# A two-layer attention and FFN kernel: the first stack by groups of heads on two DMA queues, the first weights copied on ScalarE, and products of zeros on TensorE

## The chip, the cores and the metric

The kernel runs on one core of one Trainium2 chip. The metric is the device time of one execution in microseconds; the median of the runs shown is compared. A core has TensorE (matrix products, with a separate weight load), DVE (VectorE), ACT (ScalarE), POOL (GpSimd) and SP (SyncE, which here issues the DMAs). The five engines run their own instruction streams in order and wait for each other by semaphores.

## The reference

Eight batches of 512 tokens with 256 channels (`x`) and a context of 512 tokens with 128 channels go through two layers. Every sublayer is added to `x`, and its input is normalised first.

```
x = x + L0_xattn(layernorm(x), ctx)   # causal self attention + cross attention, 16 heads of 16, then Wp
x = x + L0_ffn(layernorm(x))          # rmsnorm, int8 activations and ternary weights, 256-1024-256, gelu
x = x + L1_xattn(layernorm(x), ctx)   # cross attention, 16 heads of 16, then Wo
x = x + L1_ffn(layernorm(x))          # per-tensor int8 activations and weights, 256-1024-256, gelu
```

Attention is softmax(q k^T / 4) v for each head. All inputs and outputs are float32.

## The kernel before

**Units.** The attentions are cut into units: S (self attention of layer 0, causal), C (cross attention of layer 0) and X (cross attention of layer 1), one of each for each batch. A unit has four groups of four heads, numbered G over the whole kernel, and two halves n (u = 0, 1) of two groups each. For every half a chain of jobs runs:

- `ln_job` (line 494) loads `x` (for the first unit the tile `first_x`, loaded at line 330), takes statistics with `stats` (line 469: four `bn_stats` and four `bn_aggr` on DVE, then three small POOL operations), normalises, and transposes by products with the identity into `xlt`.
- `weights_job` (line 432) loads the q and k weights (`raw_*`, line 442; the first two already at line 337) and copies them into the order of the heads (line 449): the first four blocks on DVE, the others on POOL. After the fourth block it waits for the key `("stack", 0)` and loads the five other weights (line 456).
- `prep_job` (line 550) makes q and k of one half on TensorE (`wide`: four products of 32 columns that run side by side). ACT adds the bias, and the result is split into a high float32r part and a low remainder (`qkt`): on DVE for the first two halves (a CAST and a TENSOR_TENSOR each), on POOL after that.
- `stack_job` (line 597) copies `qkt` by six DMAs of 256 KB on SP's queue into `qk`, where every head has its high and low parts on 48 partitions. When it has done so, the keys `("stack", 2n)` and `("stack", 2n + 1)` are set.
- `max_one` (line 668) makes the scores of a pair of heads on TensorE (for S units with a mask added by two small products) and takes row maxima on DVE (`mx`).
- `rows_job` (line 706) waits for the maxima of both groups of a half, splits them into a high and a low part on POOL (`mhl`), transposes them on TensorE, evacuates them as `mrow`, and writes them by two DMAs (line 741) into partitions 48 and 49 of the q side of `qk`. Two rows of ones on the k side, written once by `init_job` (line 1361), take them into the next product.
- `exp_one` (line 756) makes the scores again, now with keys on the partitions and the maximum subtracted by those two rows, and ACT takes the exponential; `av_part` (line 804) multiplies by V.

The feed-forward network of layer 0 runs between them, and that of layer 1 at the end, after all attention.

**Order.** The whole program is written out by a planner at build time. `Plan` keeps a modelled clock for each engine and for the DMA (`run`, `op`, `pe`, `dma`), and `at` holds modelled due times by key. Jobs are generators that yield the time at which they want to go on; `until(key)` waits for a modelled time. The main loop at the end of `build` emits, at the modelled TensorE time, whichever of maxima, exponentials and products with V is ready and most urgent, and jobs between them. The emission order is the order of the instructions on every engine, so a changed due time can change the order of all that follows. The chip doesn't see the modelled times; it sees the order and the semaphores.

**Queues.** All DMAs of the kernel before are issued by SP, in emission order: at the start `x`, two weight blocks, eight small loads of biases (line 369), eight small copies of identity and mask (line 374), then two more weight blocks, then the stacks. `inputs_jobs` (line 1389) goes on to the next inputs (context and the next `x`) once `("stack", 0)` is set, and `init_job` too waits for that key.

**PSUM.** Eight banks are named `bank0` to `bank7`, and in twos `pair0` to `pair3`; `Writer.matmul` (line 259) adds waits when a bank changes its use. Nearly all instructions are recorded at a helper's line: TensorE's at 259, those of DVE and ACT at 241.

## Time and profile before

| | |
|---|---|
| median of 3 runs | 1462.89 us (1462.37 to 1465.43) |
| the profiled execution | 1460.25 us |
| its span, first to last instruction | 1458.4 us |
| mean granted TensorE clock in it | 0.971 |
| TensorE products / weight loads | 1374.8 us (94%) / 597.5 us (41%) |
| DVE / ACT / POOL busy | 1142.0 us (78%) / 1035.5 us (71%) / 681.6 us (47%) |
| DMA moved | 207.03 MB, mean 142 GB/s |
| first 64 us: TensorE / DVE / ACT busy | 43.3 / 38.3 / 13.9 us |

The span lies inside the execution's time; 1.85 us are around it. Busy time of TensorE counts overlapped products once, and a busy TensorE is not a TensorE at its peak. The clock row of the page and the clock in the stretches give the granted TensorE clock, as a share of full speed. In the timeline a line holds the start, the time it took, the engine, the line of the kernel, the operation, the tiles (written <- read), the number of merged instructions, and in brackets the idle time ahead of it and what ended that. SPq is the queue of DMA issues of SP. In the lines by shape the columns are busy time, mean of one, and idle time before it.

### The profile page before, as it was taken

How to read it: one execution, taken by the hardware profiler on the slowest of the kernel's cores; microseconds unless marked ns; L12 is line 12 of the kernel's file. 1: busy time of each engine (PE TensorE's matmuls, PEld its weight loads, DVE VectorE, ACT ScalarE, POOL GpSimd, SP SyncE). 2: the span in 40 equal slices, each digit the busy share in tenths (PEclk: the TensorE clock that was granted, in tenths of full speed). 3: DMA queues.
4: the chain of work that ended last, by engine and by line, in shares of the span. 5: the costliest groups of instructions: out<-in, count | busy, mean ns of one | idle time of the engine just before them, and what ended most of it. 6: DMA issues, size and time to landing. Idle time of an engine off the chain costs nothing. (4 is left out here: it accounts for less than half of the span.)

```text
span 1458.4 us, 36089 instructions
## 1 busy us (share of the span) xinstructions
PE 1374.8 (94%) x14400; PEld 597.5 (41%) x14400; DVE 1142.0 (78%) x1591; ACT 1035.5 (71%) x1904; POOL 681.6 (47%) x1025
## 2 busy tenths in 40 slices
PE   4999999999999999999999999999999998999978
PEld 2443444444444444434344433443333333333527
DVE  4678588697788886898777996689899888766397
ACT  1456767677768867767677777668778795777587
POOL 1463355465455465464653552654455541524332
PEclk8899999999999999999899999999999999999899
DMA  6593565667576755665457655556647657373343
GB/s 126 152 216 76 133 139 125 142 138 182 132 161 150 161 129 141 156 161 126 105 126 155 163 126 132 142 120 160 163 105 169 155 149 196 105 176 110 117 142 116
DMA packets 155612, 207.03 MB, mean 142 GB/s; under 512 B 71940, under 2 KB 74244, under 8 KB 154932
## 3 DMA queue, kind: packets, MB, share of 16 engines
q1 hardware_dynamic: 155444, 204.73, 58.0%
q8 instruction: 113, 1.85, 0.5%
q14 instruction: 55, 0.45, 0.1%
HBM read 68.15 MB, written 47.43 MB: 79 GB/s over the span
## 5 line engine op out<-in xcount | busy, mean ns | idle before, releaser
L241 DVE TENSOR_REDUCE mx<-pair 128x2 f32<-128x1024 f32 (+3 forms) x768 | 808.9, 1086 | 210.7 <-PE pair L259 194.6
L241 ACT ACTIVATE p<-bank 128x512 f32<-128x512 f32 (+1 forms) x1408 | 712.0, 587 | 232.7 <-PE bank L259 224.8
L259 PE MATMUL bank<-p,v 128*32 128x512 f32 (+3 forms) x3072 | 371.7, 563 | 2.9 <-DVE mrow L241 1.3
L259 PE MATMUL bank<-qk 50*128 50x512 f32 (+3 forms) x1536 | 337.6, 433 | 16.2 <-ACT p L241 8.0
L259 PE MATMUL pair<-qk 48*128 48x512 f32 (+3 forms) x1536 | 325.5, 438 | 25.7 <-DVE mx L241 11.8
L259 PEld LDWEIGHTS bank<-qk 50*128 50x128 f32 x1536 | 159.6, 190 | 215.7 <-ACT p L241 142.9
L259 PEld LDWEIGHTS pair<-qk 48*128 48x128 f32 x1536 | 148.0, 191 | 171.5 <-DVE mx L241 83.4
L384 POOL TENSOR_SCALAR qkt<-qkt 128x512 fp32r<-128x512 f32 x92 | 57.1, 621 | 164.1 <-ACT qkt L241 157.5
L241 ACT ACTIVATE qkt<-bank,qk_bias 128x512 f32<-128x512 f32 x96 | 66.6, 693 | 81.0 <-PE bank L259 65.4
L409 POOL TENSOR_TENSOR qkt<-qkt 128x512 fp32r<-128x512 f32 x92 | 118.8, 1291 | 7.7
L259 PEld LDWEIGHTS bank<-p,v 128*32 128x32 f32 x3072 | 70.9, 109 | 114.6 <-issue 85.9
L384 POOL TENSOR_SCALAR mhl<-mx 128x32 fp32r<-128x32 f32 x48 | 11.8, 245 | 171.3 <-DVE mx L241 164.8
L883 POOL TENSOR_TENSOR yt<-oc,rb 128x512 f32<-128x512 f32 x31 | 39.8, 1283 | 73.3 <-DMA rb<-scrz 50.9
L259 PE MATMUL pair<-mask,ident 64*128 64x128 bf16 (+2 forms) x768 | 58.0, 226 | 6.9 <-DVE mx L241 4.7
L259 PE MATMUL bank<-ident,mask 64*128 64x64 bf16 (+1 forms) x768 | 52.7, 206 | 3.7 <-ACT p L241 1.2
L259 PEld LDWEIGHTS <-ident 64*128 64x128 bf16 x768 | 26.1, 97 | 71.0 <-issue 52.8
L259 PEld LDWEIGHTS <-mask 64*128 64x128 bf16 x768 | 25.8, 96 | 69.3 <-issue 61.0
L241 ACT COPY v<-bank 128x512 f32<-128x512 f32 x44 | 26.2, 596 | 39.4 <-PE bank L259 39.1
L241 ACT COPY ev<-bank 128x512 f32<-128x512 f32 x56 | 33.5, 598 | 17.9 <-PE bank L259 17.9
L241 DVE SCALAR_TENSOR_TENSOR h<-bank,so,bc_l_b 128x512 f32<-128x512 f32 x64 | 45.3, 741 | 0.9 <-PE bank L259 0.7
L241 ACT ACT_TABLE_LOAD x34 | 43.6, 1283 | 1.9 <-PEq L1762 0.7
L1189 POOL TENSOR_SCALAR h<-h,sh 128x1024 f32<-128x1024 f32 x32 | 36.0, 1125 | 17.7 <-DVE sh L241 15.2
(230 smaller groups left out, 1686.4 us busy)
## 6 DMA issues: line engine op xcount, KB each, us to landing
qk<-qkt SPq DMA_DIRECT2D x288, 256.0 KB
scro<-ev SPq DMA_DIRECT2D x94, 256.0 KB
oc<-scro SPq DMA_DIRECT2D x47, 256.0 KB
rb<-scrz SPq DMA_DIRECT2D x47, 256.0 KB
x_d<-xb SPq DMA_DIRECT2D x15, 512.0 KB
xa_s<-in_x SPq DMA_DIRECT2D x8, 512.0 KB
xb<-in_x SPq DMA_DIRECT2D x8, 512.0 KB
xr<-x_d SPq DMA_DIRECT2D x16, 256.0 KB
```

Source lines behind the costliest of these rows:

```text
L241: r = f(*args, **kw)
L259: r = self.eng.matmul(out, *args, **kw)
L384: nc.gpsimd.tensor_scalar(dst, src, 1.0, 0.0, ALU.mult, ALU.add)
L409: nc.gpsimd.tensor_tensor(dst, full, high.bitcast(F32), ALU.subtract)
L883: nc.gpsimd.tensor_tensor(y, o, rb, ALU.mult)
L1189: nc.gpsimd.tensor_scalar(ht, ht, s[:, t - t0 : t - t0 + 1], MAGIC, ALU.mult, ALU.add)
```

## The change

- **Start.** The first `x` comes by two DMAs of 256 KB in place of one of 512 KB, and the planner lets the statistics begin when the first has landed. The copies of the first two weight blocks go to ACT (planned at 0.2 us each); the third and fourth stay on DVE.
- **Products of zeros.** `keep_warm(n)` emits n products of a 128 x 128 by a 128 x 512 bf16 operand, both broadcasts of a zero column, into the first half of `pair3`. Nobody reads them and the planner counts no time for them. Eight stand at the beginning, two wait behind each of the four first `bn_stats`, three more behind the last of these, and sixteen follow the second half's q and k products.
- **First stack.** For n = 0 the six DMAs of 256 KB become 24 of 64 KB: first the twelve of group 0 (two pairs of heads), then those of group 1, each partition half c on its own queue, SP for c = 0 and ACT for c = 1. The keys `("stack", 0)` and `("stack", 1)` are set separately. The other weights and the rows of ones wait for `("stack", 1)`, the next inputs for `("stack", 0)`. All other stacks are as they were.
- **First rows of maxima.** For n = 0 `rows_job` runs once for each group, with half-size tiles and one DMA for each c of half the rows; for every other n it runs once for both.

```diff
@@ -327,8 +327,9 @@
 
 
     first_x = tile("xa", [P, NT, C], F32, "xa_s0")
-    nc.sync.dma_start(first_x, A["x"][0])
-    at["x0"] = dma(512)
+    for t in range(0, NT, 2):
+        nc.sync.dma_start(first_x[:, t : t + 2], A["x"][0][:, t : t + 2])
+        at["x0", t] = dma(256)
     heapq.heappop(plan.rings["xa"])
     first_raw = {}
     for i, nm in enumerate(("Sq", "Sk")):
@@ -351,6 +352,19 @@
     one = const.tile([P, 1], F32, name="one")
     nc.vector.memset(one, 1.0)
     ones_sq = one.broadcast_to([P, P])
+    zero_b = zero.bitcast(BF16)[:, 0:1]
+
+    def keep_warm(n, behind=None):
+
+        for _ in range(n):
+            r = nc.tensor.matmul(
+                pairs[3][:, 0], zero_b.broadcast_to([P, P]), zero_b.broadcast_to([P, T]), start=True, stop=True
+            )
+            if behind is not None:
+                tc.add_manual_dep(r.ins, behind.ins.name, SYNC, reason="warm")
+                behind = None
+
+    keep_warm(8)
 
     ident2 = const.tile([P, 2, P], BF16, name="ident2")
     mask2 = const.tile([P, 2, P], BF16, name="mask2")
@@ -446,12 +460,15 @@
                 for h in range(2):
                     full = raw[:, k * P : (k + 1) * P].rearrange("p (g c d h) -> p h c d g", g=2, c=2, h=2)
                     dst = WT[nm][:, u, k].rearrange("p (c d g h) -> p h c d g", c=2, g=2, h=2)
-                    (nc.vector if n < 4 else nc.gpsimd).tensor_copy(dst[:, h], full[:, h])
-                    t = plan.run("dve" if n < 4 else "pool", 0.2)
+                    if n < 2:
+                        nc.scalar.copy(dst[:, h], full[:, h])
+                    else:
+                        (nc.vector if n < 4 else nc.gpsimd).tensor_copy(dst[:, h], full[:, h])
+                    t = plan.run("act" if n < 2 else "dve" if n < 4 else "pool", 0.2)
             give("oc", t)
             at["w", nm, u] = t
             if n == 3:
-                yield from until(("stack", 0))
+                yield from until(("stack", 1))
                 for v in ("Vs", "Vc", "Vx", "Wp", "Wo"):
                     nc.sync.dma_start(WT[v].rearrange("p k m -> p (k m)"), WSRC[v])
                     at["w", v] = dma(256)
@@ -473,12 +490,16 @@
         r = wp.tile([P, NT], F32, tag="rstd", name=f"r_{nm}", bufs=3)
         neg = wp.tile([P, NT], F32, tag="nmean", name=f"nm_{nm}", bufs=3)
         for t in range(NT):
-            nc.vector.bn_stats(st[:, t, :], x[:, t, :])
+            r_st = nc.vector.bn_stats(st[:, t, :], x[:, t, :])
+            if nm == "s0":
+                keep_warm(2, r_st)
             op("dve", C)
             yield plan.now + 0.4
         for t in range(NT):
             nc.vector.bn_aggr(mv[:, t, :], st[:, t, :])
         te = plan.run("dve", 0.4)
+        if nm == "s0":
+            keep_warm(3, r_st)
         nc.gpsimd.tensor_scalar(r, mv[:, :, 1], LN_EPS, 0.0, ALU.add, ALU.add)
         nc.gpsimd.tensor_tensor(r, r, mhalf, ALU.pow)
         nc.gpsimd.tensor_scalar(neg, mv[:, :, 0], -1.0, 0.0, ALU.mult, ALU.add)
@@ -497,7 +518,7 @@
             yield from until(("x3", key[1]))
         if key == ("S", 0):
             x = first_x
-            yield at["x0"] + LAT
+            yield at["x0", 0] + LAT
         else:
             yield from take("xa")
             x = tile("xa", [P, NT, C], F32, f"xa_{nm}")
@@ -586,6 +607,8 @@
                 wide(ps, WT[wname][:, u, k], xs[:, k, :], k == 0, k == nk - 1)
                 tm = plan.pe(4 * T, "cols")
             used(key, ring, tm)
+            if (n, i) == (1, 1):
+                keep_warm(16)
             ready.append((wname, ps, pb, tm, hi, lo))
             if n >= 2 or i == 1:
                 for r in ready:
@@ -601,7 +624,20 @@
         if n >= NQK:
             yield from until(("exp", 2 * (n - NQK) + 1))
         dst = qk_t[n % NQK].bitcast(F32)
-        for r, parts in enumerate((slice(0, 4, 3), slice(1, 4, 2), slice(0, 3, 2))):
+        rows = (slice(0, 4, 3), slice(1, 4, 2), slice(0, 3, 2))
+
+        for g in range(2 if n == 0 else 0):
+            for r, parts in enumerate(rows):
+                yield (at["qkt", n] if r < 2 else tl[1]) + LAT
+                for pair in (2 * g, 2 * g + 1):
+                    for c, q in enumerate((nc.sync, nc.scalar)):
+                        q.dma_start(
+                            dst[64 * c + r : 64 * c + 48 : 3, pair], tf[64 * c + pair : 64 * c + 64 : 4, parts, :]
+                        )
+                    plan.run("act", 0.65)
+                    t = dma(128, dims=3)
+            at["stack", g] = t
+        for r, parts in enumerate(rows if n else ()):
             yield (at["qkt", n] if r < 2 else tl[1]) + LAT
             for c in range(2):
                 nc.sync.dma_start(
@@ -609,7 +645,8 @@
                     tf[64 * c : 64 * c + 64, parts, :],
                 )
                 t = dma(256, dims=3)
-        at["stack", 2 * n] = at["stack", 2 * n + 1] = t
+        if n:
+            at["stack", 2 * n] = at["stack", 2 * n + 1] = t
         give("qkt", t)
 
     VW = {"S": ("Vs", "S"), "C": ("Vc", "K"), "X": ("Vx", "K")}
@@ -703,17 +740,22 @@
         if s + 1 == len(MAX_STEPS) or MAX_STEPS[s + 1][0] != G:
             at["max", G] = t
 
-    def rows_job(n):
-
-        yield from until(("max", 2 * n), ("max", 2 * n + 1))
-        m = mx_t.pop(n).rearrange("p c g t -> p t c g")
-        hl = wp.tile([P, NT, 2, 2, 4], F32R, tag="mhl", name=f"mhl{n}", bufs=1)
+    def rows_job(n, g0, ng):
+
+        yield from until(*(("max", 2 * n + g) for g in range(g0, g0 + ng)))
+        last = g0 + ng == 2
+        ps = slice(2 * g0, 2 * (g0 + ng))
+        m = mx_t[n].rearrange("p c g t -> p t c g")[:, :, :, ps]
+        hl = wp.tile([P, NT, 2, 2, 2 * ng], F32R, tag=f"mhl{ng}", name=f"mhl{n}{g0}", bufs=1)
         copy_ts(hl[:, :, :, 0], m)
         nc.gpsimd.tensor_tensor(hl[:, :, :, 1], m, hl[:, :, :, 0].bitcast(F32), ALU.subtract)
         t = plan.run("pool", 0.5)
-        give("mx", t)
+        if last:
+            del mx_t[n]
+            give("mx", t)
         yield pe_next(t)
-        row = wp.tile([16, T], F32R, tag="mrow", name=f"mrow{n}", bufs=1)
+        k = 8 * ng
+        row = wp.tile([16, T], F32R, tag="mrow", name=f"mrow{n}{g0}", bufs=1)[:k]
 
         while (t := plan.bank_at("gn", 2)) is None:
             yield plan.now + 0.2
@@ -724,14 +766,14 @@
             for h, i in enumerate(got):
                 half = slice(64 * h, 64 * h + 64)
                 nc.tensor.matmul(
-                    banks[i][:16, qt * P :][:, half], hl[half, qt].rearrange("p c a g -> p (c a g)"), ident_r[half, half],
+                    banks[i][:k, qt * P :][:, half], hl[half, qt].rearrange("p c a g -> p (c a g)"), ident_r[half, half],
                     start=True, stop=True,
                 )
         tm = plan.pe(ROW_COLS, "rows")
         t = 0.0
         for h, i in enumerate(got):
             dst, src = (
-                x.rearrange("p (t n) -> p t n", t=NT)[:, :, 64 * h : 64 * h + 64] for x in (row, banks[i][:16])
+                x.rearrange("p (t n) -> p t n", t=NT)[:, :, 64 * h : 64 * h + 64] for x in (row, banks[i][:k])
             )
             te = evacuate(dst, src, T // 2, tm)
             give_bank(i, te)
@@ -739,10 +781,12 @@
         yield t + LAT
         for c in range(2):
             nc.sync.dma_start(
-                qk_t[n % NQK].bitcast(F32)[64 * c + 48 : 64 * c + 50, :, 0], row.bitcast(F32)[8 * c : 8 * c + 8]
+                qk_t[n % NQK].bitcast(F32)[64 * c + 48 : 64 * c + 50, ps, 0],
+                row.bitcast(F32)[k // 2 * c : k // 2 * c + k // 2],
             )
             t = dma(16, dims=3)
-        at["rows", 2 * n] = at["rows", 2 * n + 1] = t
+        for g in range(g0, g0 + ng):
+            at["rows", 2 * n + g] = t
 
     p_t, p_at, p_slots, av_t, scr_o = {}, {}, {}, {}, {}
 
@@ -1359,7 +1403,7 @@
 
 
     def init_job():
-        yield from until(("stack", 0))
+        yield from until(("stack", 1))
         yield from take("ev")
         ones = tile("ev", [4, T], F32, "ones_rows")
 
@@ -1397,7 +1441,8 @@
             if kind == "X":
                 yield from ln_job(("X", b), lambda b=b: x3_d[b], f"x{b}", 2)
 
-    plan.start(series(rows_job(n) for n in range(2 * NU)), 0)
+    rows = [(0, 0, 1), (0, 1, 1)] + [(n, 0, 2) for n in range(1, 2 * NU)]
+    plan.start(series(rows_job(*r) for r in rows), 0)
     plan.start(series(evac_job(G) for G in range(NG - 2)), 0)
     plan.start(weights_job(), 0)
     plan.start(inputs_jobs(), 1)
```

## The prediction

> **What bounds the kernel now.** I read the page's busy shares and clock row first, then busy time by stretch, then the timeline of the first 64 us, since every edit lies there.
>
> ```profile
> PE 1374.8 (94%) x14400; PEld 597.5 (41%) x14400; DVE 1142.0 (78%) x1591; ACT 1035.5 (71%) x1904; POOL 681.6 (47%) x1025
> PEclk8899999999999999999899999999999999999899
> ```
>
> TensorE is busy 94%. From 60 to 1380 us the stretch view gives it 1271.3 of 1320 us, so only 48.7 us of idle are left in the steady part. Whatever TensorE loses ahead of that part is therefore time of the whole kernel, and I count an edit by the TensorE time it gives back before 64 us.
>
> The stretches (PE, PEld, DVE, ACT, POOL busy, then granted clock, DMA share, GB/s):
>
> ```profile
> 24.50:28.80 4.30, 0.48 (x3) 0.33 (x3) 0.00 (x0) 0.00 (x0) 0.00 (x0) 0.50 1.07 180
> 28.80:38.25 9.45, 7.93 (x57) 5.90 (x57) 8.12 (x12) 0.00 (x0) 0.00 (x0) 0.50 1.07 230
> 38.25:43.10 4.85, 4.85 (x46) 2.08 (x44) 3.02 (x4) 0.00 (x0) 0.00 (x0) 0.50 0.70 251
> 54.40:56.02 1.62, 0.00 (x0) 0.00 (x0) 1.62 (x8) 0.00 (x0) 1.05 (x2) 1.00 0.00 0
> 56.02:63.24 7.22, 7.22 (x66) 4.26 (x65) 6.03 (x9) 4.34 (x9) 5.92 (x18) 0.56 0.06 14
> ```
>
> Here TensorE waits for the stack's DMA; then DVE's maxima are the limit (8.12 of 9.45 us) at half clock; then TensorE is, still at half clock; at 54.4 it waits for DVE; and it runs at half clock again to 63.2.
>
> The timeline (start, us, engine, line, what):
>
> ```profile
> 12.40 0.53 SPq L442 DMA_DIRECT2D raw_Sq<-in_wa  x1
> ...
> 14.74 0.54 DVE L241 COPY w_Sq<-raw_Sq 128x64 f32<-128x64 f32 x4 [4.66 <-DMA raw_Sq<-in_wa]
> ...
> 17.49 9.00 SPq L607 DMA_DIRECT2D qk<-qkt  x12
> ...
> 27.27 0.47 PE L259 MATMUL pair<-qk 48*128 48x128 f32 x1 [7.31 <-DMA qk<-qkt]
> ...
> 28.79 0.87 PE L259 MATMUL pair<-qk 48*128 48x128 f32 x3 [1.05 <-issue]
> ...
> 29.70 3.08 DVE L241 TENSOR_REDUCE mx<-pair 128x2 f32<-128x256 f32 x5 [8.07 <-PE pair L259]
> ...
> 48.30 1.31 SPq L741 DMA_DIRECT2D qk<-mrow  x2
> ...
> 56.38 0.50 PE L259 MATMUL bank<-qk 50*128 50x512 f32 x2
> ```
>
> The first stack is issued from 17.49, its two halves land at 27.27 and about 28.8, the first maximum starts at 29.70, its rows go out at 48.30, the first exponentials' scores run at 56.38.
>
> **Part by part.**
>
> *Split of x, weight copies on ScalarE, 19 products at the start.* The two copies between DVE's statistics cost 0.52 us each; without them, and with half of x earlier, the aggregate (6.55) comes some 1.4 us sooner, and so does normalising (8.70). But none of it reaches the stack: DVE is in order, and ahead of the first qkt CAST (15.63) stand the copies of the second weight blocks, which wait for a load that SP issues at 12.40, after 16 small DMAs back to back from 2.13. Splitting x adds one SP issue of 0.42 us: load 12.8, landed 15.1 (12.40 to 14.74 took 2.3), copies to 16.1, then CAST, TENSOR_TENSOR, CAST (0.42, 0.69, 0.43): first stack DMA at 17.7, 0.2 us later than now. ScalarE's eight copies (0.2 us each by DVE's row) hide in its idle time before 11.16. If the cover were gone, that is if the second blocks' copies stood behind the CASTs, 1.4 us would be won.
>
> The zero products are weighed against the clock row, which says 1.00 from 0 to 20 us, so that they would be worth nothing. The Trainium skill (TensorE: Matmul & The Clock Gate, "What's actually happening") says the reverse: the throttled state is the default, and activity releases it. Rows of one shape decide, the first transposes and those at 64.9 to 68.3 us:
>
> ```profile
> L259 PE MATMUL bank<-ident_r,xa_s 128*32 128x128 f32 x64 | 3.6, 414 | 9.2 <-DVE xa_s L241 9.2
> ...
> L259 PE MATMUL bank<-ident_r,xa_s 128*32 128x128 f32 x64 | 2.1, 274 | 0.0
> ```
>
> They agree with the page, not with the clock row: 414 ns against 274, so the start is cold, and warming saves 1.5 us on TensorE. It goes into the same wait of DVE. Taken: the second projection ends 0.3 us earlier (19.4 for 19.7), **-0.3**; ends -1.5 and +0.4.
>
> *First stack by groups, two queues.* Six DMAs of 256 KB become 24 of 64 KB, 12 for each group of heads, half on each queue. SP's issue has a median of 0.65 us, 0.72 from start to start. ScalarE issues no DMA in this trace: the nearest row is SP's same DMA; ends 0.4 (SP's plainest issues) and 1.0 (its longest, 1.011). At 0.72 the sixth of each queue starts at 17.7 + 5 x 0.72 = 21.3 and lands 2.3 later, 23.6. By bytes: 0.79 MB at 190 GB/s from 19.2 (bytes move 1.5 us after the issue) is 23.3, plus the 1.6 us by which landing (28.7) now trails the bytes (27.1): 24.9. I take 24.4. The skill has a rule against the two queues (DMA: Bandwidth & Descriptors, "Issuing engines are not separate DMA queues"): all run on the same 16 engines, a second issuer saves only issue time. The trace agrees on the bytes (DMA share 1.07 with one queue), but here issue time counts: 12 DMAs on SP alone are 8.6 us, landing at 28 and gaining nothing; on two queues the pairs come at 182 GB/s, just the transfer rate. TensorE's wait of 8.8 us (19.95 to 28.79) becomes 4.9: **-3.9**; with an issue of 1.0 us -2.5.
>
> *16 zero products behind the second projection.* No row has this shape; the page's 216 ns for 512 columns gives 3.45 us as an estimate, 19.4 to 22.9, inside the wait. By the same page's rule (no gap over some 3 us) the clock then stays up, which would be worth half of the 4.85 us from 38.25, 2.4 us. But the trace's stretch from 53.5 to 56.9, 1.78 of 3.4 us busy, is followed by the drop at 56.9. The maxima of the first two groups take DVE 13.1 us (4.8 + 3.8 + 2.8 + 1.7, by width, between 29.5 and 45.6) and TensorE at full clock about 6.9 (0.69 + 0.46 + 0.58 a pair in the timeline from 44.9 to 50.9, four pairs): 53% again. I take the row: only the first products are warm, **-0.1**, the drop comes some windows later.
>
> *What the stack's issues push back.* ScalarE's 12 issues run 17.7 to 26.3; behind them stand the second unit-half's two activations (now 18.03 and 19.75), then DVE's four qkt steps (2.2 us): done near 30 instead of 21.6. And the planner's "stack 0" key now means the first group, earlier, while the weights wait for "stack 1" and so come before the second stack: SP passes ctx, the next x, five weights, raw Cq (1.9 MB, at the 340 to 410 GB/s of 36 to 40 us: 5 us) and the rows of ones (six of 0.62) first. SP also seems to hold eight DMAs in flight: the 13th since the stack began goes at 27.24, as the fifth lands. The second stack then issues from 33, moves 1.57 MB in 8.3 us, lands about 44.4 against 36.8 now. DVE ends the first two groups at 24.8 + 13.1 + 2.2 = 40.1 (now 45.2), waits, and starts the third at 44.6 (now 45.6). While it waits TensorE has work that now lies after 43: V and Cq projections, whose weights come earlier. From 24.4 to 44.5 it does 6.9 + 8.3 (V four times 1.07, Cq 2.1, the next V 1.9, at full clock) of 20.1 us; now, from 28.8 to 45.2, 6.9 + 3.2 (three V) + 1.4 (two steps of the third group), 11.5 of 16.4. Lost both times: 4.9. **0**; ends -3 and +5.
>
> *Rows by group.* The first group's maxima end at 33.6, rows on ScalarE by 35.2 (POOL's two steps 0.5, possibly behind its weight copies), their DMA behind the second stack on SP: issued 38.5, landed about 44.5. Exponentials run from 46 instead of 56.4. They fill the idle of 54.4 (1.6), and of the 3.2 us lost to the clock from 56 to 63 I take a third, 1.0: **-2.6**; ends 0 and -4.8. Added work: eight small transposes (0.3 us), two copies and two DMAs: **+0.6** with their waits.
>
> Sum: -0.3 - 3.9 - 0.1 + 0 - 2.6 + 0.6 = -6.3. The profiled execution took 1460.25 (span 1458.4 and 1.85 around it): it would be 1454.0. The median of the runs is 1462.89, 2.6 above; against it the forecast is **1456.6**.
>
> **Rivals.** *More* (0.12): group 0's rows slip ahead of the second stack on SP, exponentials run from 37, ScalarE, idle from 20.4 to 43.6 today, feeds TensorE, and both half-clock stretches go (2.4 + 3.2): 1450. Against it: SP's order. *Given back* (0.18): all later order is written by the planner from shifted clocks, and the 48.7 us idle of the steady part are dealt anew; a tenth more of them eats 5 us: 1461.5. For it: DVE idles from 63 to 80 for the third stack in any case. Against it: there TensorE has other work. *Slower* (0.18): the second stack comes too late. Its place is ScalarE's queue and then SP's; at 1.0 us an issue ScalarE is free at 30, DVE stands at its qkt CAST, and the second stack lands at about 52. It decides from about 50: until then the first two groups' exponentials and products feed TensorE. Past it DVE, then TensorE stand 5 us, and the gain of the stack is gone too: 1468. *Does not do what it says*: landing at 28, were ScalarE's issues serial with SP's; 1462, counted with the third.
>
> **Numbers.** Forecast 0.52, its own range 1453 to 1460. The rest as given. Measurement tells 0.2%, 2.9 us. Faster than 1460: 0.12, most of 0.52, little else: 0.63. Within: 0.19. Slower than 1465.8: 0.18. The range 1450 to 1468 reaches both outer cases' centres and leaves out half of each and little besides, under 0.2.
>
> **What would show it.** First CAST at 16.1, not earlier (else the start gives 1.4). First maximum's product near 24.4, first reduction before 25.5. ScalarE without activations from 17.7 to 26. Second stack after the weights on SP, landed by 45. First exponential near 46. TensorE busy by 64 us some 6 us of full-clock work further. Transposes at 274 ns from the first. Wrong if the granted clock never falls (better), or if TensorE's idle between 60 and 1380 moves by more than 5 us either way.

## The result and the profile after

The change made the kernel slower: 1471.98 us (median of nine, 1466.12 to 1480.08) against 1462.37 us for the kernel before beside it (nine, 1458.65 to 1470.64), a ratio of 1.0061 with a 95% interval of 1.0032 to 1.0090. The forecast was 1456.6. The profiled execution of the changed kernel took 1466.12 us, the fastest of its nine, with a span of 1464.3. It also has the highest granted clock of the nine (0.974; the others 0.960 to 0.972) and is 5.9 us slower than the profiled execution before, where the medians differ by 9.6: some 4 us of the loss are not in this profile.

The page of the kernel after, busy shares and clock row:

```profile
PE 1377.5 (94%) x14436; PEld 597.8 (41%) x14443; DVE 1139.0 (78%) x1583; ACT 1039.1 (71%) x1914; POOL 679.3 (46%) x1027
PEclk8999999999999999999999999999999999899999
```

Nothing here looks slower than before: the mean clock is 0.974 (0.971 before), and TensorE's busy time is longer by 2.7 us, less than the 9.1 us that the zeros take in the records. The loss has to be looked for in time. First the start, from the timeline of the kernel after (start, us, engine, line, what, idle before it and its releaser):

```profile
1.66 5.70 PE L259 MATMUL pair<-zero 128*128 128x512 bf16 x19 [1.66 <-DVE one L241]
...
16.25 0.53 DVE L241 COPY w_Sq<-raw_Sq 128x64 f32<-128x64 f32 x4 [7.65 <-DMA raw_Sq<-in_wa]
...
17.14 0.42 DVE L241 CAST qkt<-qkt 128x512 fp32r<-128x512 f32 x1
...
18.65 8.10 SPq L634 DMA_DIRECT2D qk<-qkt  x12
18.65 7.78 ACTq L241 DMA_DIRECT2D qk<-qkt  x12
...
20.50 3.45 PE L259 MATMUL pair<-zero 128*128 128x512 bf16 x15 [0.16 <-issue]
...
24.39 0.62 PE L259 MATMUL pair<-qk 48*128 48x128 f32 x4 [0.17 <-DMA qk<-qkt]
...
25.05 2.49 DVE L241 TENSOR_REDUCE mx<-pair 128x2 f32<-128x256 f32 x4 [5.71 <-PE pair L259]
...
26.48 1.26 ACT L241 ACTIVATE qkt<-bank,qk_bias 128x512 f32<-128x512 f32 x2 [12.29 <-DMA qk<-qkt]
...
35.07 4.44 SPq L643 DMA_DIRECT2D qk<-qkt  x6
...
39.61 1.40 SPq L783 DMA_DIRECT2D qk<-mrow  x2
...
48.57 1.29 DVE L241 TENSOR_REDUCE mx<-pair 128x2 f32<-128x256 f32 x2 [4.36 <-PE pair L259]
49.15 4.03 ACT L241 ACTIVATE p<-bank 128x512 f32<-128x512 f32 x8 [0.59 <-PE bank L259]
```

The first product of the maxima runs at 24.39 (27.27 before), the first reduction at 25.05 (29.70), the first rows go out at 39.61 (48.30), the first exponentials run at 49.15 (56.89). The head start is there. Then it is lost. The timeline of the kernel after, 62 to 90 us:

```profile
65.67 5.34 SPq L643 DMA_DIRECT2D qk<-qkt  x6
...
69.76 0.24 POOL L398 TENSOR_SCALAR mhl<-mx 128x32 fp32r<-128x32 f32 x1
...
73.48 1.76 SPq L783 DMA_DIRECT2D qk<-mrow  x2
76.05 0.69 PE L259 MATMUL pair<-qk 48*128 48x512 f32 x1 [4.59 <-DMA qk<-qkt]
...
86.06 4.06 ACT L241 ACTIVATE p<-bank 128x512 f32<-128x512 f32 x8
```

and of the kernel before:

```profile
66.14 3.72 SPq L607 DMA_DIRECT2D qk<-qkt  x4
...
70.69 1.39 SPq L741 DMA_DIRECT2D qk<-mrow  x2
...
73.54 1.64 ACT L241 ACTIVATE p<-bank 128x512 f32<-128x512 f32 x4 [1.79 <-PE bank L259]
76.07 1.70 ACT L241 ACTIVATE p<-bank 128x256 f32<-128x256 f32 x4
```

The third stack (the first half of the next unit) is issued at about 66 us in both. Before, TensorE and ScalarE still have exponentials of the first half to do then. After, those were done by 61.9; TensorE's order puts a product of the third stack next, and it stands for it 4.59 us, the clock falls to half at 76.2 for 6.8 us, and ScalarE has no exponential for 24 us, until 86.06. The second half's rows, which the head start was to help, go out at 73.48, later than the 70.69 of before.

To add this up I use one sum throughout: what TensorE has lost up to a moment is its idle time, plus half of its busy time at half clock, plus the time of the products of zeros, all from the records of one profiled execution. It leaves out the cold start, where the granted clock reads 1.00 (the first transposes keep TensorE busy for 3.6 us before and 2.3 after). Carried to the end it says 8.7 us for a span that is 5.9 longer, so it is good to some 3 us.

| TensorE's loss (us) up to | 60 | 80 | 120 | 240 | 260 | 360 us |
|---|---|---|---|---|---|---|
| kernel before | 28.9 | 31.5 | 32.7 | 36.0 | 37.9 | 40.7 |
| kernel after | 23.5 | 30.1 | 35.3 | 39.8 | 45.9 | 48.2 |
| after, without the zeros | 20.2 | 27.7 | 30.1 | 32.5 | 39.5 | 42.3 |
| before, first stack's due time 4 us earlier | 28.4 | 32.7 | 35.8 | 37.6 | 44.5 | 47.1 |
| old order, first stack on SP and POOL, `w_Vs` first | 25.4 | 25.9 | 26.7 | 31.1 | 34.3 | 36.9 |

By 60 us the change has won 5.4 us, zeros counted against it. By 80 it holds 1.4, by 120 it is 2.6 behind, and a second step of 4 us is lost between 240 and 260. The views of both stretches (PE, PEld, DVE, ACT, POOL busy, then granted clock, DMA share, GB/s), first the kernel after, then the one before:

```profile
60.00:120.00 60.00, 52.87 (x548) 22.28 (x548) 46.00 (x62) 26.82 (x56) 39.44 (x60) 0.92 0.67 150
240.00:260.00 20.00, 16.43 (x188) 7.42 (x180) 13.20 (x22) 17.54 (x29) 5.30 (x8) 0.83 0.69 150
...
60.00:120.00 60.00, 58.94 (x669) 24.94 (x667) 42.71 (x63) 35.12 (x75) 37.20 (x60) 0.96 0.71 170
240.00:260.00 20.00, 18.11 (x220) 7.78 (x212) 14.68 (x23) 18.15 (x31) 8.87 (x13) 1.00 0.68 146
```

In the second step TensorE waits, in the kernel after,

```profile
248.11 0.39 PE L259 MATMUL bank<-ident_r,mhl 64*16 64x64 f32 x7 [2.46 <-ACT p L241]
```

and in the kernel before, at the same place,

```profile
245.90 1.07 PE L259 MATMUL bank<-p,v 128*32 128x512 f32 x8 [1.31 <-DVE mrow L241]
```

followed after by 6.8 us at half clock from 246.9, before by none. The order of TensorE's instructions is the same in both kernels from about 263 us on.

The profiles of the experiments below say how much of this is the order. Twelve profiles have the old order (the kernel before and eleven experiments). From 60 to 120 us they lose 1.3 to 4.3 us; the three with the order of the change lose 9.9 to 11.8. One of the three, the order alone, has hardly any head start (27.0 us lost by 60), so the first step goes with the order. The second does so only in part: from 235 to 262 us TensorE is idle for 1.9 to 2.1 us in all twelve and for 3.3 to 3.6 in those three, but a half-clock stretch begins near this place in ten of the twelve too. The kernel before, as profiled, is one of the two that it missed.

The line that answers the transposes (by shape; busy, mean ns, idle before), the first ones after:

```profile
L259 PE MATMUL bank<-ident_r,xa_s 128*32 128x128 f32 x64 | 2.3, 279 | 0.3 <-DVE xa_s L241 0.3
```

279 ns in place of 414: the first zeros warm TensorE, as the Trainium skill has it (TensorE: Matmul & The Clock Gate, "What's actually happening": activity releases a throttled default), although the granted clock reads 1.00 there in both kernels.

### The profile page after: what moved, and what is told of

Read it like the earlier page. It is cut to its first block, busy times and chain, and to the rows that moved or that the text cites. A ratio compares the mean times of both kernels' runs of the same rounds, so it can differ in the third digit from the quotient of the medians.

```text
span 1464.3 us, 36212 instructions
## 1 busy us (share of the span) xinstructions
PE 1377.5 (94%) x14436; PEld 597.8 (41%) x14443; DVE 1139.0 (78%) x1583; ACT 1039.1 (71%) x1914; POOL 679.3 (46%) x1027
## 4 chain that ended last, share of the span: by engine, by line
PE 66%; DMA 10%; DVE 9%; ACT 8%; issue 2%; SPq 2%; POOL 2%; ACTq 0%; DVEq 0%; POOLq 0%
PE bank L259 53%; PE pair L259 13%; DMA qk<-qkt 5%; DVE mx L241 5%; ACT p L241 3%; DVE gmax L241 2%; SPq L643 2%; DMA hqt<-hq 2%; DMA qk<-mrow 2%; ACT L241 1%; ACT jq L241 1%; ACT h L241 1%; DMA tyt<-tyq 0%; DVE am L241 0%; ACT gq L241 0%
## 5 line engine op out<-in xcount | busy, mean ns | idle before, releaser
L259 PE MATMUL bank<-p,v 128*32 128x512 f32 (+3 forms) x3072 | 367.6, 558 | 1.6 <-ACT ev L241 0.9
L398 POOL TENSOR_SCALAR qkt<-qkt 128x512 fp32r<-128x512 f32 x92 | 57.8, 628 | 166.9 <-ACT qkt L241 141.3
L398 POOL TENSOR_SCALAR mhl<-mx 128x32 fp32r<-128x32 f32 (+1 forms) x49 | 11.8, 242 | 166.0 <-DVE mx L241 159.6
L259 PE MATMUL pair<-mask,ident 64*128 64x128 bf16 (+2 forms) x768 | 57.8, 225 | 7.3 <-DVE mx L241 4.3
L259 PE MATMUL bank<-l0w,hqt 128*32 128x256 bf16 x1024 | 37.9, 274 | 2.4 <-DMA hqt<-hq 2.3
```

Source lines behind the costliest of these rows:

```text
L259: r = self.eng.matmul(out, *args, **kw)
L398: nc.gpsimd.tensor_scalar(dst, src, 1.0, 0.0, ALU.mult, ALU.add)
```

## The experiments

Every kernel here computes the whole result; products of zeros are extra work that nobody reads. Ratios are to the kernel before beside it, with 95% intervals. At first there were three theories. ORDER: the planner deals the later order anew, and that order is worse. QUEUES: the stack's issues on ScalarE and the load order on SP cost more than they bring. ZEROS: the products of zeros cost.

**The change without the zeros.** The four `keep_warm` calls are left out; the order is that of the change.

```
-    keep_warm(8)
...
-                keep_warm(2, r_st)
...
-            keep_warm(3, r_st)
...
-                keep_warm(16)
```

> The change without any product of zeros; the order of all other instructions is that of the change. Three theories. ORDER (what costs is the order that the planner writes for the first 260 us once the due times of the first stack have moved): as slow as the change, 1.003 to 1.009 of before, first exponentials about 1 us later than the 49.2 us of the change. QUEUES (what costs are the 12 issues on ScalarE and the second stack that they push back): the same, 1.003 to 1.009. ZEROS (the 35 products take TensorE time or its clock at a bad moment): back to 0.998 to 1.001. All: transposes at the start at 414 ns again in place of some 274.

Measured: 1466.55 us, 1.0024 [1.0009, 1.0039]. By the medians the zeros carry over half of the loss (5.4 us of 9.6), though the two intervals overlap a little; what is left is still slower.

**The start alone.** The kernel before with x in two halves and the first two weight blocks on ScalarE:

```
+    for t in range(0, NT, 2):
+        nc.sync.dma_start(first_x[:, t : t + 2], A["x"][0][:, t : t + 2])
...
+                    if n < 2:
+                        nc.scalar.copy(dst[:, h], full[:, h])
```

> Before with only x in two DMAs and the first two weight blocks copied on ScalarE; the order of TensorE, POOL and SP is that of before. ORDER, QUEUES and ZEROS all: 0.999 to 1.001. The first stack is issued between 17.7 and 18.7 us (17.49 before), because the second weight blocks are loaded one SP issue later and DVE's copies of them stand ahead of its CAST; a start below 17 us would say that DVE's order does not hold it.

Measured: 1462.21 us, 0.9997 [0.9980, 1.0015]; first CAST at 16.10, first stack DMA at 17.61 (17.49 before). Worth nothing, for the reason that the prediction gave: the copies of the second blocks stand ahead of the CAST.

**The order alone.** Order and rows by groups as in the change, but no start edits, no zeros, and the first stack as six DMAs of 256 KB on SP:

```
-                for pair in (2 * g, 2 * g + 1):
-                    for c, q in enumerate((nc.sync, nc.scalar)):
-                        q.dma_start(dst[... pair], tf[... parts, :])
+                for c in range(2 if g == 0 else 0):
+                    nc.sync.dma_start(dst[...], tf[64 * c : 64 * c + 64, parts, :])
```

> The order of the change without its work: x in one DMA, weight copies on DVE, no zeros, the first stack as six DMAs of 256 KB on SP, but all that follows in the order that the planner writes for the change, rows of the first half by groups. ORDER: at least as slow as the change, 1.003 to 1.010, since the stack also lands later. QUEUES: 0.998 to 1.002. ZEROS: 0.998 to 1.002.

Measured: 1469.68 us, 1.0054 [1.0038, 1.0069]. The new order without the faster start costs 7.1 us.

**The change planned as before.** All that the change does on the chip, zeros too, but due times as in the kernel before and rows joint, so that TensorE's order is the old one:

```
-            at["stack", g] = t
...
+        at["stack", 2 * n] = at["stack", 2 * n + 1] = t
...
-    rows = [(0, 0, 1), (0, 1, 1)] + [(n, 0, 2) for n in range(1, 2 * NU)]
+    rows = [(n, 0, 2) for n in range(2 * NU)]
```

> All of the change as work on the engines (split x, copies on ScalarE, zeros, the first stack by groups in 24 DMAs on two queues), but planned with the due times of before, and the rows of maxima of the first half in one go as before, so that the order on every engine is that of before. ORDER: 0.997 to 1.001 of before, since the order is the old one and the first stack still lands 4 us earlier. QUEUES: 1.003 to 1.009, since ScalarE's issues and the late second activation are all there. ZEROS: 1.003 to 1.009.

Measured: 1474.23 us, 1.0078 [1.0051, 1.0106]. So ORDER alone can't be the cause. The next run takes the zeros out of this one.

**The same without zeros.**

> The start edits (x in two halves, first weights copied on ScalarE) and the first stack through two queues, without the 35 zero products, the rows joint and the order of every engine's work planned as in the kernel before. ZEROS (the products of zeros cost some 5 us by themselves, by way of later half-clock stretches, in any order): 0.996 to 1.000, and clearly under the same order with zeros (1.0078). QUEUES (the stack's issues on ScalarE hold up the second half's activations, which costs more than the earlier landing gives): 1.004 to 1.008. ORDER alone (only the re-planned order costs): 0.997 to 1.000, so it does not tell ZEROS from ORDER; the run with the zeros alone does.

Measured: 1465.74 us, 1.0011 [0.9989, 1.0033]. The zeros cost 0.7% in the old order too. And the stack on two queues wins nothing there; its timeline says why:

```profile
17.61 7.77 ACTq L241 DMA_DIRECT2D qk<-qkt  x12
...
25.43 1.26 ACT L241 ACTIVATE qkt<-bank,qk_bias 128x512 f32<-128x512 f32 x2 [10.16 <-DMA qk<-qkt]
26.14 0.43 DVE L241 CAST qkt<-qkt 128x512 fp32r<-128x512 f32 x1 [7.84 <-ACT qkt L241]
...
28.28 3.08 DVE L241 TENSOR_REDUCE mx<-pair 128x2 f32<-128x256 f32 x5
```

TensorE has the first scores at 23.33, but in this order DVE has to split the second half's q and k first, and they wait behind ScalarE's twelve issues: the first reduction is only 1.4 us earlier than before.

**The zeros alone.** The kernel before with the 35 zeros at the same places.

```
+    keep_warm(8)
...
+                keep_warm(2, r_st)
...
+            keep_warm(3, r_st)
...
+                keep_warm(16)
```

> The kernel before with the 35 products of zeros put in at the same four places, and nothing else: their result is not read, and the order of all else stays. ZEROS: 1.003 to 1.006, with the first stack's DMA going out later than 17.5 us and the loss made of half-clock stretches after 60 us. If zeros in a wait are free: 0.998 to 1.001. If they do what warming should do: transposes at about 274 ns for one instead of 414, the clock at half later than 22.8 us, and 0.997 to 0.999.

Measured: 1468.29 us, 1.0037 [1.0018, 1.0057]. The transposes are warm (279 ns) and the first stack's DMA is 0.35 us later, as expected. The half clock begins at 25.3 and not 22.8, but it does so at 25.3 with a single narrow zero as well (below), so it need not be an effect of these products. But the first exponentials are within 0.4 us of those before.

**The first 19, and the last 16.** Two kernels, each with a part of these zeros.

> The kernel before with the first 19 products of zeros alone (at the start, up to the transposes); they are not read. If the cost of the 35 (1.0037) comes from the start, where they push the first stack's DMA back by 0.35 us: 1.002 to 1.004, and the other 16 alone nothing. If it goes by the number of products: 1.001 to 1.003.

> The kernel before with the last 16 products of zeros alone (behind the second projection, in TensorE's wait for the first stack); they are not read. If zeros in a wait are free: 0.999 to 1.001. If the cost goes by the number of products: 1.001 to 1.003. If these 16 carry it all: 1.003 to 1.006.

Measured: 1469.89 us, 1.0050 [1.0026, 1.0075], and 1468.10 us, 1.0042 [1.0020, 1.0064]. Either part costs about as much as all 35. The cost does not add up by number.

**Sixteen narrow ones, a single one, and 32.** The products behind the second projection, with 2 columns in place of 512, and with twice the number:

```
-                pairs[3][:, 0], zero_b.broadcast_to([P, P]), zero_b.broadcast_to([P, T]), ...
+                pairs[3][:, 0, :2], zero_b.broadcast_to([P, P]), zero_b.broadcast_to([P, 2]), ...
```

> The kernel before with 16 products of zeros of 2 columns each (instead of 512) behind the second projection; they are not read. ACTIVITY (what costs is what TensorE does in its wait): with next to no work in them 0.999 to 1.001. STREAM (what costs is that instructions are added to TensorE's stream at all, which shifts everything behind them): 1.003 to 1.005, as with the 16 of 512 columns (1.0042).

> The kernel before with a single product of zeros of 2 columns, not read: the nearest thing to the same kernel again. ACTIVITY: 0.999 to 1.001. STREAM: 1.000 to 1.005. It also shows what the measurement itself makes of a kernel that differs in nothing that lasts.

> The kernel before with 32 products of zeros of 512 columns behind the second projection (twice the 16), which just fill TensorE's wait of 7.3 us for the first stack; they are not read. ACTIVITY: about twice the 16, 1.006 to 1.009, and the clock at full for the first maxima. STREAM: as the 16, 1.003 to 1.005.

Measured: 16 narrow 1468.79 us, 1.0029 [1.0007, 1.0051]; one 1462.56 us, 0.9986 [0.9969, 1.0003]; 32 wide 1470.40 us, 1.0044 [1.0024, 1.0064]. The timeline with 32:

```profile
19.48 6.95 PE L259 MATMUL pair<-zero 128*128 128x512 bf16 x31 [0.16 <-issue]
...
26.93 0.32 PE L259 MATMUL pair<-qk 48*128 48x128 f32 x1 [0.23 <-DMA qk<-qkt]
```

They end before the stack lands, and the first score isn't later than before. Twice the products cost no more, and next to no work in them costs, by the median, over half as much, with a wide interval. ACTIVITY as a proportional cost is out; that added instructions cost by being in the stream fits five of six runs, and the single one costs nothing. What in them costs is not settled: no row of waits in the profiles carries it. TensorE's waits add up to 75.2 us before and to 69.9 to 75.6 in the five profiles of this order with 16 zeros or more. The half clock carries a part. The record has the mean granted clock of every timed run, and twice its shortfall from 1, times the span, estimates the time at half clock; half of that is at most what it cost. Against the kernel before beside them the five kernels have more of this cost by 0.2 us (35 zeros), 5.2 (first 19), 1.6 (last 16), 4.5 (16 narrow) and 0.7 (32), each to about 1.5 us either way, where their mean times are longer by 4.6, 7.0, 5.1, 5.0 and 6.5. So in two of them it could be most of the cost, and in three it is little.

**The second stack first.** The change without zeros, its five weight loads behind the second stack:

```
-                yield from until(("stack", 1))
+                yield from until(("stack", 2))
```

> The change without the zero products, with the second half's stack issued ahead of the five weight loads (their due time now waits for the second stack); the planner then writes the first tenth of the order anew. LATE STACK (the lead of the exponentials is lost because the third group's maxima start at 48.6 us and the second half's rows go out at 73.5): third group's first reduction at 40 to 42 us, second half's rows out by 66, TensorE's stand of 4.6 us at 71.5 gone, and 3 to 5 us off the change without zeros, that is 0.998 to 1.000. ORDER in general (any re-dealt order loses some 5 us somewhere): 1.002 to 1.006 all the same, with the earlier stack given back elsewhere.

Measured, in five executions: 1477.69 us, 1.0104 [1.0067, 1.0141]. The first exponential ends at 44.6, 13 us earlier than before, the third group's first reduction at 43.42, and the kernel is slower than the change. The third stack now goes out at 78.58 (64.85 without this edit), and TensorE loses 12.3 us between 80 and 120, 5.3 of them idle, mostly in waits for DVE, and 7.0 at half clock:

```profile
78.58 5.12 SPq L636 DMA_DIRECT2D qk<-qkt  x6
...
99.77 0.51 PE L259 MATMUL pair<-qk 48*128 48x512 f32 x2 [0.63 <-DVE mx L241]
101.49 0.79 PE L259 MATMUL pair<-qk 48*128 48x512 f32 x2 [1.22 <-DVE mx L241]
```

The theory that the late second stack eats the gain has fallen: mended, the loss comes elsewhere, and larger.

**The third stack earlier.** The change without zeros, the copies of Cq and Ck on ScalarE; and the same copies alone on the kernel before:

```
-                    if n < 2:
+                    if n < 2 or 4 <= n < 8:
                         nc.scalar.copy(dst[:, h], full[:, h])
```

> The change without the zero products, and the eight weight copies of the next stage's first projections (Cq, Ck) on ScalarE instead of POOL, so that the third stack can be ready earlier; the order behind it is planned anew. WALL (the head start is lost because the third stack is issued at 65 us whatever the first one does): third stack issued by 60 us, TensorE's idle between 60 and 80 us below 2 us instead of 5.1, its loss by 120 us 3 to 5 us less than in the change without zeros, and 0.996 to 0.999 of the time before. ORDER (any newly dealt order loses about 5 us elsewhere): 1.002 to 1.006 even if the third stack is earlier.

> The kernel before with only those eight copies (Cq, Ck) moved from POOL to ScalarE, order planned anew behind 40 us. WALL: in the old order TensorE has other work at 62 to 80 us (0.7 us idle), so an earlier third stack wins nothing there: 0.998 to 1.001. ORDER: 1.002 to 1.006. A gain of more than 0.2% would say that the third stack bounds the old order too.

Measured: 1475.80 us (six executions), 1.0105 [1.0064, 1.0145], and 1465.89 us, 1.0011 [0.9988, 1.0034]. The first is a miss as a test: its third stack went out at 65.14, no earlier. What it shows is another newly dealt order that costs: 0.8% more than the change without zeros, whose physical work is nearly the same. By the granted clock of the timed runs this kernel and the one before it in this list are at half clock for about 116 us an execution, against about 90 for the kernel before: that could be up to 13 of the 14 us by which their mean times are longer.

**Only the due time.** The kernel before with nothing altered but the planner's belief of when the first stack is done:

```
-        at["stack", 2 * n] = at["stack", 2 * n + 1] = t
+        at["stack", 2 * n] = at["stack", 2 * n + 1] = t + (-4.0 if n == 0 else 0.0)
```

> The kernel before with nothing changed but the planner's belief: the first stack's due time 4 us earlier, about as in the change. The same instructions in another order over the first 170 us, the same order behind. ORDER (any order dealt anew loses some 5 us against the one of before): 1.002 to 1.006. If a new order is as likely to win as to lose: 0.998 to 1.002.

> The kernel before with nothing changed but the planner's belief: the first stack's due time 2 us later; the first 170 us in another order, the same behind. ORDER (a newly dealt order loses): 1.002 to 1.006, as the run with 4 us earlier (1.0044). If that run was one bad draw among even ones: 0.998 to 1.002.

Measured: 4 us earlier 1470.12 us, 1.0044 [1.0022, 1.0065]; 2 us later 1462.93 us, 1.0003 [0.9982, 1.0024]. One new order is 6.7 us worse, one even: dealing the order anew does not always cost. None of the seven kernels here with a newly dealt order has a better median than the kernel before. The loss up to 360 us of the first is in the table above; from 60 to 120 us it loses 7.5 us, and it has the same step between 240 and 260 as the change.

**The old order with POOL's queue.** As the old order without zeros, but the second queue is POOL's, which is idle then:

```
-                for c, q in enumerate((nc.sync, nc.scalar)):
+                for c, q in enumerate((nc.sync, nc.gpsimd)):
```

> The order of the kernel before on every engine, with the start edits and the first stack through two queues without the zero products, but the second queue is POOL's, which has nothing to do from 13 to 45 us, instead of ScalarE's. QUEUES (on ScalarE the issues held up the second half's activations, so DVE began its maxima only at 28.3 us): second half's CASTs at 19 to 21 us again, first reduction at 24 to 26 us instead of 28.3, first exponentials at 53 to 55 instead of 58.8, and 0.996 to 0.999. If a head start before 60 us is worth nothing at the end whatever the order: 0.999 to 1.001. If POOL's issues are slower than ScalarE's 0.65 us: first product later than 26 us and 1.000 to 1.003.

Measured: 1462.62 us, 1.0000 [0.9977, 1.0023]. The first reduction is at 24.66, as expected, but the first exponential ends only 1.4 us earlier than the mean of four old-order profiles (before, start alone, ScalarE's queue, zeros alone: 57.8). The timeline shows where it went:

```profile
36.86 1.94 PE L259 MATMUL bank<-w_Vs,xlt_s 128*32 128x256 f32 x16 [3.57 <-DMA w_Vs<-in_wv]
...
39.49 2.00 DVE L241 TENSOR_REDUCE mx<-pair 128x2 f32<-128x512 f32 x2 [5.17 <-PE pair L259]
```

TensorE's wait for the stack has turned into a wait for `w_Vs`, issued at 29.89 behind both stacks.

**`w_Vs` first.** The same, with that load ahead of the first stack:

```
+                if n == 3:
+                    nc.sync.dma_start(WT["Vs"].rearrange("p k m -> p (k m)"), WSRC["Vs"])
```

> The run with POOL's queue once more, with one load moved: w_Vs is issued on SP before the first stack, behind raw_Sk, and no longer behind the second stack. All else keeps the order of the kernel before. In the run with POOL's queue the wait for the first stack had gone and TensorE stood 3.57 us for w_Vs instead. If that wait is what ate the gain: it goes, DVE's 5.2 us idle before 39.5 shrinks below 2, the first exponentials come at 52 to 54 us, and 0.996 to 0.999. If the head start is eaten by the next limit (the half clock to 43 us, then the third stack): TensorE's loss by 120 us as with POOL's queue (30.0 us) within 1.5 us, and 0.999 to 1.001.

Measured: 1461.27 us beside 1460.85, 0.9984 [0.9963, 1.0005]. The timeline:

```profile
32.89 1.93 PE L259 MATMUL bank<-w_Vs,xlt_s 128*32 128x256 f32 x16
...
35.51 2.00 DVE L241 TENSOR_REDUCE mx<-pair 128x2 f32<-128x512 f32 x2 [1.53 <-PE pair L259]
```

The wait is gone, DVE's is 1.53, and the first exponential ends 5.6 us earlier than that mean. By the times at which SP writes the rows of maxima, this profile is 5.8 us ahead of the mean of those four at about 230 us, 6.2 at 1200 and 4.6 at 1337. Against the profile of the kernel before alone it is 6.7, 2.7 and 0.4 us ahead, and the run with POOL's queue, in the same order, is 3.9 us behind the mean at 1337. So a head start can last in an unchanged order, but these single profiles don't show that it does. The profiled execution, 1457.52 us, is the fifth fastest of twelve, and the times show 0.16% with an interval that includes no change. It is the only version with the earlier stack whose best estimate is ahead of the kernel before; that it beats it is not shown.

## Why the prediction was wrong

The sum of the prediction was a sum up to 64 us, and that part held but for the zeros.

- *Start, -0.3.* First CAST foretold at 16.1: 16.10 in the run with the start alone, 17.14 in the profile of the change, where the small mask DMAs ahead of the weight load took SP 3.52 us in place of 2.46; in the run without zeros they are again as before and the CAST is at 16.15. Nothing won, as said.
- *First stack on two queues, -3.9.* First product foretold at 24.4, measured 24.39, although the stack started 0.95 us later than foretold: 5.74 us from first issue to first product, against 9.8 before. ScalarE issues at 0.65 us each (7.78 for twelve), as SP does; that estimate was right. The Trainium skill's warning (DMA: Bandwidth & Descriptors, "Issuing engines are not separate DMA queues") that a second issuer saves no more than issue time did not decide: issue time was the part that counted here.
- *Sixteen zeros, -0.1: wrong.* Their length (3.67 us for 16 in the old order, estimate 3.45) was right, and so was that they lie in a wait. The half clock begins at 28.4 us in the change and at 22.8 without the zeros, later as foretold, but its start also differs between kernels without them (21.7 to 24.6). That nothing else follows from them was not: between the medians they cost 5.4 us in the order of the change and 4.4 to 8.5 in the old one. The step counted only what they do in the stretch where they lie and gave nothing for what follows, and no rival had it.
- *What the stack's issues push back, 0.* ScalarE was free at 26.4 (26.3 foretold). The second stack went at 35.07 (33), the third group's maxima began at 48.57 (44.6), 4 us later. But by 60 us this did no harm: TensorE had its other work.
- *Rows by group, -2.6.* Rows at 39.61 (38.5 foretold), exponentials at 49.15 (46). All together, 5.4 us were won by 60 us, 8.7 in the run without the zeros, where 6.3 were foretold.
- *The step that failed* is the one from there to the end: "Whatever TensorE loses ahead of that part is therefore time of the whole kernel". It can be so only if what follows is done in the same order. Here the same edits dealt the order anew, and this was given no cost in the sum. The prediction named the sign: TensorE's idle time between 60 and 1380 us moving by more than 5 us. It went from 48.7 to 58.4, and is 54.3 without the zeros and 59.8 with the order alone, while it is 47.1 to 50.4 in eleven of the twelve profiles of the old order (54.1 in the last run's). *Given back* named the mechanism and was put at 0.18, on the ground that TensorE has other work from 63 to 80 us. That is read from the old order. In the new one that work was done earlier (the first exponentials start at 53.6 us even with the order alone, at 56.9 before), and TensorE stood 4.59 us for a third stack whose own chain nobody had moved. The order alone costs 7.1 us (1.0054); by the medians the faster start pays 3.1 of it back, and the zeros' 5.4 come on top.
- *Slower* was a rival with the second stack as its mechanism, deciding from a landing at 50 us. That is not what happened, and sending that stack first made it worse. That its 1468 lies nearest to the measured time is luck.

Open are what in the added zeros costs, and why one order is worse than another beyond the stretch from 60 to 120 us. That the loss there, in the kernel after, comes from the third stack is read from one order's profile: the run that was to bring that stack earlier did not do so.

## What to carry to other kernels

Where a planner writes the order, an edit to a due time is an edit to all that follows: time the edit once with the old order kept and once with the new, before either is credited. A stage that gets ahead need not keep its lead if the next input comes by a chain that was not moved: follow that chain to its issue, and look whether the work that covered it before has already been done. And work that fills a wait isn't free because the profile shows it inside the wait; compare timed runs with and without it.

## What the runs showed of the hardware

- Products of zeros in TensorE's waits, unread and off the path, cost 0.3 to 0.5% here in five kernels of the old order, about as much for 16 as for 35; with 2 columns 1.0029, with 512 1.0042. A single one cost nothing (0.9986 [0.9969, 1.0003]). The cause isn't known.
- In these profiles the half-clock stretches are multiples of 3.41 us long (3.4, 6.8, 10.2, 13.7, 20.5), and within an execution they start whole multiples of that apart: before, 22.8, 56.9 and 118.4 us, 10 and 28 steps. The phase differs between executions: 22.8 before, 21.7 with the start alone, 24.6 with ScalarE's queue in the old order. In the same order they fall at the same places (near 244, 383, 458, 708, 746, 960, 1240 us), but which of these places are hit, and for how long, differs from one profile to the next. That moves a profile's progress by up to 4 us either way with the same order, so one profile cannot judge 5 us at the end.
- Within one kernel, execution time goes with the granted clock: in the largest set of the kernel before (55 timed runs) the correlation of time with the time at half clock is 0.83.
- POOL issued twelve DMAs of 64 KB in 6.21 us (run with POOL's queue), ScalarE in 7.78 and SP in 8.10 (the change).
